# Graph attention in two layers: the opening reordered round x and the queries' weights, row sums on another engine, multiplications by zeros, a fold moved behind the second scores

## The chip, the cores and the metric

The kernel runs on one core of a Trainium2 chip. A core has a matrix engine (TensorE, PE in the profile, with its weight loads as PEld), a vector engine (VectorE, DVE), a scalar engine for activations (ScalarE, ACT), a general engine (GpSimd, POOL) and a queue that issues transfers (SyncE, SP), all working side by side and held together by semaphores. Matmul results land in PSUM, which this kernel cuts into eight banks; everything else lies in SBUF. The metric is the device time of one execution in microseconds (us), lower is better.

## The reference

The input x has 32 batches of 512 rows by 512 columns, and adj is a 512 by 512 matrix of zeros and ones. The first layer is attention with eight heads of 64, masked by adj, with a residual and a layer norm; the second multiplies by adj and by a weight matrix, again with a residual and a norm. All in float32.

```python
q = (x @ Wq + bq); k = (x @ Wk + bk); v = (x @ Wv + bv)      # split into 8 heads of 64
scores = einsum('bihd,bjhd->bhij', q, k) / sqrt(64)
weights = softmax(scores + where(adj == 0, -1e9, 0), axis=-1)
x = layernorm(x + einsum('bhij,bjhd->bihd', weights, v))
y = einsum('nm,bmd->bnd', adj, x)
x = layernorm(x + einsum('bnd,do->bno', y, weight) + bias)
```

## The kernel before

**Order.** The order of all instructions is written out by hand: each engine runs its own list in the order of the program text, and SP issues its transfers in that order too. `run(units)` simply calls a list of units one after the other. Tiles come from pools with a fixed number of buffers; a tile waits for the last reader of the buffer that it takes. PSUM banks go round in a ring of eight.

**Projections.** A projection multiplies 512 by 512 matrices by Strassen's scheme in Winograd's form: seven products of half-size blocks instead of eight. The left side's sums of blocks (S1, S2, S3, S4) lie in the tile `xT`, which holds x turned over; the right side's sums (T1, T2, T3, T4) lie in the weight tile (`wq`, `wk`, `wv`, `w1`). `sum_weights(w, n)` (L319) makes one of the four weight sums on VectorE: n = 0 makes T1, n = 1 makes T3, n = 2 makes T2, n = 3 makes T4, and T2 reads T1. `combine` makes all four and subtracts the halves of the bias (L326). `combine_rows` (L331 to L333) makes S2, S3 and S4 on POOL. `project(b, which, i)` does product i (L369, four matmuls, eight records in the trace, two for each) and takes the result out of its bank: products 1 and 5 with the bias (L394 on ACT for q and k, L391 on DVE for v), the others by additions on DVE (L397, L399, L404), with two additions on POOL after product 7 (L400, L401). The products come in the order 1, 5, 6, 7, 2, 3, 4. Product 5 reads S1 and T1, 6 reads S2 and T2, 7 reads S3 and T3, 3 reads S4, 4 reads T4; 1 and 2 read no sums.

**The opening.** SP issues, in this order: the four blocks of x's first batch (`xin`), the two halves of `wq`, `bq_c`, the two halves of `wk`, `bk_c`, `adj_s` (in the tile yT), the two halves of `wv`, `bv_r`, sixteen small transfers for the second batch (`load_squares(1)`, which need the four `xin` buffers back), the residual rows of batch 0 (`xs`), `w1`, `b1_r` and the rows of batch 1. PE turns each block of x over (`x_transpose`: four transposes, L342; eviction on ACT, L344; S1 for blocks 2 and 3 on DVE, L346), then runs the projections of batch 0, with `combine(wq)` ahead of them, `combine(wk)` after the first five products and `combine(wv)` after nine. Between them lie the transposes of adj (L301, L302, L303). The last units of the opening are the first scores, the rest of v, and the postponed additions of exponentials.

**Attention.** The heads are worked on in pairs (hp), two pairs to a group (b, g), two groups to a batch. `scores` does, for each pair and each of four blocks, two matmuls (L568), two masked copies out of the banks on DVE (L570) and one exponential on ACT (L572); POOL adds the exponentials up in `es` (L583). `attend` multiplies them by v (L592). `fold_squares` turns `es` over on DVE (L623, into a tile named e with eight buffers) and sums it (L625) into `part`; `add_up` makes the row sums across partitions on PE (L633) and their inverses on DVE (L636, L637) and POOL (L638). `turn_out` turns the result over on DVE (L606, into one of two buffers named attT) and has SP write it into `rows` by sixteen transfers (L611). `scale_rows` and `add_rows` later scale and add these.

The main loop goes through the groups: for each of the two pairs attend, fold and turn out, then the next group's scores, `add_up`, then the group's slot, a list of units made of the next batch's projections with other work merged between them. In the first group, `flips(1)` (four transposes on DVE, L353, and the sums on POOL) runs after the first pair. In the second group's slot of batch 0 lie four looks at adj (L308 on ACT, L310 and L311 on DVE), whose scratch tile is attT too.

Of the kernel before, what the change touches and what calls it, by code (L numbers as in the profile page):

```python
# [37 lines left out]
FP = mybir.dt.float32  # L38
# [3 lines left out]
AF = mybir.ActivationFunctionType  # L42
# [5 lines left out]
P = 128  # L48
# [8 lines left out]
A_AT = {"A11": 0, "A12": 1, "A21": 2, "S3": 2, "A22": 3, "S1": 4, "S2": 5, "S4": 6}  # L57
# [7 lines left out]
def load_row(nc, pool, v, name):  # L65
    t = pool.tile([P, v.shape[0]], FP, name=name)
    nc.sync.dma_start(t, bass.AP(tensor=v.tensor, offset=v.offset, ap=[[0, P], [1, v.shape[0]]]))
    return t


def load_col(nc, pool, v, name):
    t = pool.tile([P, v.shape[0] // P], FP, name=name)
    nc.sync.dma_start(t, v.rearrange("(c p) -> p c", p=P))
    return t
# [133 lines left out]
def fast_kernel(ctx: ExitStack, tc, verdict, x, adj, Wq, bq, Wk, bk, Wv, bv, W1, b1, out):  # L208
    nc = tc.nc
    B, N, D = x.shape  # L210
    H = Wq.shape[1] // HD
    HP = H // 2
    NB = N // P
# [4 lines left out]
    consts = ctx.enter_context(tc.tile_pool(name="consts", bufs=1))  # L218
    work = ctx.enter_context(tc.tile_pool(name="work", bufs=2))
# [3 lines left out]
    def bank(*shape):  # L223

        return psum.tile([P, *shape], FP, name="bank", tag="bank", bufs=8)
# [3 lines left out]
    half = N // 2  # L229

    def load(b):
        X[b] = work.tile([P, NB, D], FP, name="xT" if b == B - 1 > 1 else "xs", bufs=1 if b == B - 1 > 1 else 2)
        nc.sync.dma_start(X[b], x[b].rearrange("(c p) d -> p c d", p=P))
# [7 lines left out]
    def load_squares(b):  # L241


        for d in range(DB):
            IN[b, d] = work.tile([P, N // SQ, SQ], FP, name="xin", bufs=XIN)
            for i in range(P // SQ):
                cols = x[b, :, d * P + i * SQ:d * P + (i + 1) * SQ]
                nc.sync.dma_start(IN[b, d][i * SQ:(i + 1) * SQ, :, :], cols.rearrange("(j r) f -> r j f", r=SQ))

    def load_factors(w, name):  # L250
        t = consts.tile([P, 7, 2, half], FP, name=name)
        for s in range(2):
            nc.sync.dma_start(t[:, 2 * s:2 * s + 2, :, :].rearrange("p a c f -> p (a c) f"),
                              w[:, s * half:(s + 1) * half].rearrange("(c p) f -> p c f", p=P))
        return t

    load_blocks(0)
    wq = load_factors(Wq, "wq")
    bq_c = load_col(nc, consts, bq, "bq_c")
    wk = load_factors(Wk, "wk")  # L260
    bk_c = load_col(nc, consts, bk, "bk_c")
    adj_s = work.tile([P, NB, N], FP, name="yT", bufs=1)
    nc.sync.dma_start(adj_s, adj.rearrange("(c p) m -> p c m", p=P))
    wv = load_factors(Wv, "wv")
    bv_r = load_row(nc, consts, bv, "bv_r")
    if B > 1:
        load_squares(1)
    load(0)
    w1 = load_factors(W1, "w1")
    b1_r = load_row(nc, consts, b1, "b1_r")  # L270
    if B > 1:
        load(1)

    ident = consts.tile([P, P], FP, name="ident")
    make_identity(nc, ident)
    ones = consts.tile([P, 1], FP, name="ones")
# [37 lines left out]
    XT, QT, KT, V = {}, {}, {}, {}  # L314

    def sum_weights(w, n):

        b11, b21, b12, b22, t1, t2, t4 = (w[:, i, :, :] for i in range(7))
        nc.vector.tensor_sub(*((t1, b12, b11), (b12, b22, b12), (t2, b22, t1), (t4, b21, t2))[n])  # L319

    def combine(w, bias):

        for n in range(4):
            sum_weights(w, n)
        width = bias.shape[1] // 2
        nc.vector.tensor_sub(bias[:, width:], bias[:, width:], bias[:, :width])  # L326

    def combine_rows(t):

        a11, a12, a21, _, s1, s2, s4 = (t[:, i, :, :] for i in range(7))  # L330
        nc.gpsimd.tensor_sub(s2, s1, a11)  # L331
        nc.gpsimd.tensor_sub(a21, a11, a21)
        nc.gpsimd.tensor_sub(s4, a12, s2)  # L333

    def x_transpose(b, c):

# [18 lines left out]

    def sum_rows(b):
        xt = XT[b]
        if b:
            nc.gpsimd.tensor_add(xt[:, A_AT["S1"], :, :], xt[:, A_AT["A21"], :, :], xt[:, A_AT["A22"], :, :])
        combine_rows(xt)  # L360

    def block_product(pm, t, w, i, turned=False):
# [43 lines left out]
    def flips(b):  # L406

        return [(turn_squares if b else x_transpose, b, c) for c in range(NB)] + [(sum_rows, b)] if b < B else []

    def projections(b):  # L410


        if b >= B:
            return []
        units = [(project, b, which, i) for which in "qkv" for i in ORDER]
        for n in (5, 12):
            units[n:n + 4] = units[n + 2:n + 4] + units[n:n + 2]
        return units
# [166 lines left out]
    def attend(b, hp):  # L585
        po = bank(N)
        for j in range(NB):
            e = E.pop((b, hp, j))
            for s in range(2):
                h = 2 * (hp % 2) + s  # L590
                values = V[b][hp // 2][:, j, h * HD:(h + 1) * HD]
                nc.tensor.matmul(po[s * HD:(s + 1) * HD, :], values, e[:, s, :],  # L592
                                 start=(j == 0), stop=(j == NB - 1))
        if (b, hp // PAIRS) != (B - 1, HP // PAIRS - 1):
            SQUARES[b, hp] = work.tile([P, 2, N], FP, name="e", bufs=8)
        OUT[b, hp] = po

    def turn_out(b, hp):
# [29 lines left out]
    def add_up(b, g):  # L628

        part = PART.pop((b, g)).rearrange("p h (j i) -> p i j h", i=P // SQ)  # L630
        pm = bank(NB, GROUP)
        for i in range(P // SQ):
            nc.tensor.matmul(pm[i * SQ:(i + 1) * SQ, :, :], fold, part[:, i, :, :], start=True, stop=True,  # L633
                             tile_position=(0, i * SQ))
        inverse = INVERSE[b, g] = work.tile([P, NB, GROUP], FP, name="inverse")
        nc.vector.reciprocal(inverse, pm)  # L636
        nc.vector.tensor_add(sums, pm, sums)  # L637
        nc.gpsimd.tensor_add(inverses, inverses, inverse)  # L638
# [39 lines left out]
    def run(units):  # L678
        for unit in units:
            unit[0](*unit[1:])  # L680

    run(flips(0))
    combine(wq, bq_c)
    first = projections(0)
    run(first[:5])
    combine(wk, bk_c)
    run(first[5:9])
    combine(wv, bv_r)
    for c in range(NB):
# [74 lines left out]
    for i, (b, g) in enumerate(groups):  # L764
        for hp in range(g * PAIRS, (g + 1) * PAIRS):
            attend(b, hp)
            if i < len(groups) - 1:
                fold_squares(b, hp)
            turn_out(b, hp)
            if i == hp == 0:  # L770
                run(flips(1))
        if g == 0:
            slots = units_of(b)
        if i < len(groups) - 1:
            later = scores(*groups[i + 1])
            add_up(b, g)
        if g == 0 and b + 2 < B:
            load_squares(b + 2)
        for unit in slots[g]:
            run([unit])  # L780
            if unit[0] == convolve or unit[0] == project and unit[3] == 7:
                run(later)
                later = []
        run(later)
        later = []
# [83 lines left out]
```

## Time and profile before

| | us |
|---|---|
| median of three runs | 2764.36 (2764.18 to 2764.61) |
| the profiled execution | 2764.78 |
| span of the profiled execution, first to last instruction | 2762.9 |
| first transposes of x begin on PE | 3.71 |
| first product begins | 8.47 |
| wk's second product begins | 22.38 |
| first scores begin on PE | 41.58 |
| second scores begin on PE | 64.56 |
| PE waits for the values of batch 1 | 126.35 to 131.02 |

The profile's page gives the busy time of each engine, a picture of the span in slices, the transfers, the chain of work that ended last, and the costliest groups of instructions. The trace behind it can be asked for the instructions of any stretch in order of time, for groups by line, and for the busy time and clock of each engine in a stretch. A line of the page names source line, engine, operation, the tile written and the tiles read, how many, busy time and mean length, and the idle time before them with what ended it. The landing of each transfer is a semaphore event: the four blocks of x had landed at 3.58, 4.20, 5.80 and 6.87, the halves of wq at 8.34 and 9.78, bq_c at 10.48, the halves of wk at 11.96 and 13.59.

The last part of the page lists the transfers (tile from tensor, queue, count, size of one, us from issue to landing):

```profile
xin<-in_x_dram SPq DMA_DIRECT2D x4, 256.0 KB, 3.6
wq<-in_L_gnn_Wq_dram SPq DMA_DIRECT2D x2, 512.0 KB, 6.2
wk<-in_L_gnn_Wk_dram SPq DMA_DIRECT2D x2, 512.0 KB, 8.2
yT<-in_adj_dram SPq DMA_DIRECT2D x1, 1024.0 KB, 7.9
```

### The profile page before, as it was taken

What the parts mean: (1) busy time and instruction counts of PE and PEld (TensorE: products, weight loads), DVE (VectorE), ACT (ScalarE), POOL (GpSimd) and SP (SyncE); (2) the same over time, 40 slices, a digit from 0 to 9 for tenths busy, and PEclk for the clock granted to TensorE, in tenths of its full rate; (3) what the DMA queues carried; (4) which work ended last, traced back from release to release, by engine and by line L of the source; (5) the groups of instructions that cost most, each with busy time, mean ns of one, the idle gap of its engine ahead of it and who ended that gap; (6) DMA issues with size and microseconds to landing.
All of it is one profiled execution on the core that took longest, in us unless ns stands there. A gap on an engine that the chain in (4) does not pass through costs nothing.

```text
span 2762.9 us, 39328 instructions
## 1 busy us (share of the span) xinstructions
PE 2735.6 (99%) x12842; PEld 1912.7 (69%) x12842; DVE 2068.2 (75%) x3347; ACT 1411.1 (51%) x2459; POOL 1902.6 (69%) x1223
## 2 busy tenths in 40 slices
PE   9999999999999999999999999999999999999997
PEld 6666766767767667677676676776766767767665
DVE  6777777787777777777777777777777777787777
ACT  2455544655545546445554465454554544655554
POOL 4666777667767667676677776776666867667774
PEclk9999999999999999999999999999999999999999
DMA  5122212222122222122221222211222212222121
GB/s 147 29 31 57 45 30 56 60 60 56 25 49 58 61 56 36 38 56 62 58 53 21 56 59 60 56 26 48 58 62 57 44 30 56 61 58 57 26 51 49
DMA packets 592915, 142.20 MB, mean 51 GB/s; under 512 B 554560, under 2 KB 558656, under 8 KB 592704
## 3 DMA queue, kind: packets, MB, share of 16 engines
q1 hardware_dynamic: 592704, 139.63, 23.1%
q8 instruction: 103, 1.69, 0.3%
q14 instruction: 108, 0.88, 0.1%
HBM read 72.88 MB, written 33.55 MB: 39 GB/s over the span
## 4 chain that ended last, share of the span: by engine, by line
PE 97%; DVE 1%; SPq 1%; ACT 0%; DMA 0%; issue 0%; POOL 0%; DVEq 0%; ACTq 0%
PE bank L369 55%; PE bank L568 16%; PE bank L592 16%; PE bank L488 8%; SPq L611 1%; PE bank L633 0%; DVE bnst L431 0%; DMA wq<-in_L_gnn_Wq_dram 0%; ACT rows L649 0%; PE bank L515 0%; DVE xT L541 0%; DVE part L816 0%; DVE xs L541 0%; DVE xT L506 0%; DVE low L503 0%
## 5 line engine op out<-in xcount | busy, mean ns | idle before, releaser
L572 ACT ACTIVATE e<-e 128x1024 f32<-128x1024 f32 x512 | 524.6, 1053 | 581.3 <-DVE e L570 559.5
L570 DVE SCALAR_TENSOR_TENSOR e<-gap,bank 128x512 f32<-128x512 uint8 x1024 | 617.9, 681 | 20.2 <-PE bank L568 20.2
L583 POOL TENSOR_TENSOR es<-es,e 128x1024 f32<-128x1024 f32 x256 | 618.2, 2415 | 20.1
L583 POOL TENSOR_TENSOR es<-e 128x1024 f32<-128x1024 f32 x128 | 315.9, 2468 | 333.0 <-ACT e L572 333.0
L568 PE MATMUL bank<-q,k 64*128 64x512 f32 x2048 | 465.2, 599 | 0.0
L592 PE MATMUL bank<-e,v 128*64 128x512 f32 x2048 | 456.5, 598 | 4.7 <-DVE v L404 4.7
L369 PE MATMUL bank<-wv,xT 128*128 128x256 f32 x1792 | 405.4, 381 | 0.0
L369 PE MATMUL bank<-xT,wk 128*128 128x256 f32 x1792 | 403.0, 379 | 0.7 <-DVE wk L319 0.7
L369 PE MATMUL bank<-xT,wq 128*128 128x256 f32 x1792 | 403.1, 383 | 0.4 <-DMA wq<-in_L_gnn_Wq_dram 0.4
L369 PE MATMUL bank<-w,yT 128*128 128x256 f32 x1792 | 392.3, 379 | 0.5 <-DVE yT L520 0.5
L568 PEld LDWEIGHTS bank<-q,k 64*128 64x128 f32 x2048 | 204.0, 186 | 259.6 <-issue 160.4
L369 PEld LDWEIGHTS bank<-w,yT 128*128 128x128 f32 x1792 | 340.0, 190 | 48.1 <-DVE yT L520 0.9
L369 PEld LDWEIGHTS bank<-xT,wk 128*128 128x128 f32 x1792 | 340.2, 190 | 47.2 <-PE bank L369 1.1
L369 PEld LDWEIGHTS bank<-xT,wq 128*128 128x128 f32 x1792 | 339.5, 191 | 47.4 <-ACT xT L344 0.8
L369 PEld LDWEIGHTS bank<-wv,xT 128*128 128x128 f32 x1792 | 337.5, 190 | 47.5 <-DVE e L570 0.8
L649 ACT ACTIVATE rows<-rows,zero,inverse 128x64 f32<-128x64 f32 x1008 | 343.2, 427 | 0.0
L592 PEld LDWEIGHTS bank<-e,v 128*64 128x64 f32 x2048 | 142.2, 137 | 283.8 <-issue 282.7
L653 POOL TENSOR_TENSOR xs<-xs,rows 128x512 f32<-128x512 f32 x124 | 158.4, 1289 | 168.0 <-DMA xs<-in_x_dram 168.0
L572 ACT ACT_TABLE_LOAD x30 | 38.5, 1283 | 423.9 <-DVE e L570 423.9
L461 DVE TENSOR_TENSOR low<-xs,high 128x512 fp32r<-128x512 f32 x122 | 143.5, 1176 | 104.2 <-ACT high L457 104.2
L446 ACT ACTIVATE xs<-xs,shift,rstd 128x512 f32<-128x512 f32 x248 | 181.9, 803 | 32.5 <-DVE shift L441 32.5
L541 DVE TENSOR_TENSOR xs<-bank,xs 128x512 f32<-128x512 f32 x186 | 124.5, 683 | 96.9 <-PE bank L369 46.5
(122 smaller groups left out, 2970.1 us busy)
## 6 DMA issues: line engine op xcount, KB each, us to landing
rows<-attT SPq DMA_DIRECT2D x2016, 16.0 KB, 1.8
xin<-in_x_dram SPq DMA_DIRECT2D x496, 64.0 KB, 2.5
xs<-in_x_dram SPq DMA_DIRECT2D x31, 1024.0 KB, 5.2
out_dram<-xs SPq DMA_DIRECT2D x31, 1024.0 KB, 4.4
xin<-in_x_dram SPq DMA_DIRECT2D x4, 256.0 KB, 3.6
wq<-in_L_gnn_Wq_dram SPq DMA_DIRECT2D x2, 512.0 KB, 6.2
wk<-in_L_gnn_Wk_dram SPq DMA_DIRECT2D x2, 512.0 KB, 8.2
yT<-in_adj_dram SPq DMA_DIRECT2D x1, 1024.0 KB, 7.9
```

Source lines behind the costliest of these rows:

```text
L369: nc.tensor.matmul(pm[:, r, :], left[:, d, r * P:(r + 1) * P], right[:, d, :], start=(d == 0), stop=(d == 1))
L446: nc.scalar.activation(row, row, AF.Identity, bias=SHIFT[t][:, slot:slot + 1], scale=RSTD[t][:, slot:slot + 1])
L461: nc.vector.tensor_sub(LOW[b, d], cols, HIGH[b, d].bitcast(FP))
L488: nc.tensor.matmul(pm.rearrange("p a n -> p (a n)"), part, adjT[:, n % NB, :], start=(n == 0), stop=(n == 2 * NB - 1))
L541: nc.vector.tensor_add(block, pm, block)
L568: nc.tensor.matmul(ps[s], keys[:, j * P:(j + 1) * P], queries, start=True, stop=True)
L570: nc.vector.scalar_tensor_tensor(e[:, s, :], gap[:, j, :], NEG * root, ps[s], op0=ALU.mult, op1=ALU.add)
L572: nc.scalar.activation(e, e, AF.Exp, scale=1.0 / root)
L583: nc.gpsimd.tensor_add(ES[b, hp], ES[b, hp] if j > 1 else E[b, hp, 0], E[b, hp, j])
L592: nc.tensor.matmul(po[s * HD:(s + 1) * HD, :], values, e[:, s, :], start=(j == 0), stop=(j == NB - 1))
L649: nc.scalar.activation(part, part, AF.Identity, bias=zero, scale=inverse[:, c, s:s + 1])
L653: nc.gpsimd.tensor_add(cols, cols, ROWS.pop((b, hp)))
```

## The change

Five things change; what is computed does not.

1. Seven matmuls of a 128 by 128 tile of zeros (`still`) with itself stand at the head of PE's list. VectorE sets the tile to zero. Nothing reads their result.
2. Only x's first blocks and wq (and bq_c) are issued at once. Every other transfer is issued later in the program text, and the first of them, wk, has to wait: ScalarE writes one column of the tile wk after the eviction of x's third block, and the transfer overwrites it.
3. The row sums S2, S3, S4 of the first batch are made on VectorE, alternating with the weight sums in the order T1, S2, T2, S3, T3, S4; T4 and the bias follow after the first product, and wk's T1 is made after the third, ahead of the other wk sums. S1 of the first batch is still made by `x_transpose`.
4. In the first group, the second pair's fold moves behind the second scores; it writes into a buffer named v (three buffers) in place of e.
5. In the first group, `add_up` moves into the slot, in front of its ninth unit (after five projections of batch 1).

```diff
--- before.py
+++ after.py
@@ -247,8 +247,9 @@
                 cols = x[b, :, d * P + i * SQ:d * P + (i + 1) * SQ]
                 nc.sync.dma_start(IN[b, d][i * SQ:(i + 1) * SQ, :, :], cols.rearrange("(j r) f -> r j f", r=SQ))
 
-    def load_factors(w, name):
-        t = consts.tile([P, 7, 2, half], FP, name=name)
+    def load_factors(w, name, t=None):
+        if t is None:
+            t = consts.tile([P, 7, 2, half], FP, name=name)
         for s in range(2):
             nc.sync.dma_start(t[:, 2 * s:2 * s + 2, :, :].rearrange("p a c f -> p (a c) f"),
                               w[:, s * half:(s + 1) * half].rearrange("(c p) f -> p c f", p=P))
@@ -256,21 +257,6 @@
 
     load_blocks(0)
     wq = load_factors(Wq, "wq")
-    bq_c = load_col(nc, consts, bq, "bq_c")
-    wk = load_factors(Wk, "wk")
-    bk_c = load_col(nc, consts, bk, "bk_c")
-    adj_s = work.tile([P, NB, N], FP, name="yT", bufs=1)
-    nc.sync.dma_start(adj_s, adj.rearrange("(c p) m -> p c m", p=P))
-    wv = load_factors(Wv, "wv")
-    bv_r = load_row(nc, consts, bv, "bv_r")
-    if B > 1:
-        load_squares(1)
-    load(0)
-    w1 = load_factors(W1, "w1")
-    b1_r = load_row(nc, consts, b1, "b1_r")
-    if B > 1:
-        load(1)
-
     ident = consts.tile([P, P], FP, name="ident")
     make_identity(nc, ident)
     ones = consts.tile([P, 1], FP, name="ones")
@@ -318,19 +304,18 @@
         b11, b21, b12, b22, t1, t2, t4 = (w[:, i, :, :] for i in range(7))
         nc.vector.tensor_sub(*((t1, b12, b11), (b12, b22, b12), (t2, b22, t1), (t4, b21, t2))[n])
 
-    def combine(w, bias):
-
-        for n in range(4):
+    def combine(w, bias, which=range(4)):
+
+        for n in which:
             sum_weights(w, n)
         width = bias.shape[1] // 2
         nc.vector.tensor_sub(bias[:, width:], bias[:, width:], bias[:, :width])
 
-    def combine_rows(t):
+    def combine_rows(t, engine=nc.gpsimd, which=range(3)):
 
         a11, a12, a21, _, s1, s2, s4 = (t[:, i, :, :] for i in range(7))
-        nc.gpsimd.tensor_sub(s2, s1, a11)
-        nc.gpsimd.tensor_sub(a21, a11, a21)
-        nc.gpsimd.tensor_sub(s4, a12, s2)
+        for n in which:
+            engine.tensor_sub(*((s2, s1, a11), (a21, a11, a21), (s4, a12, s2))[n])
 
     def x_transpose(b, c):
 
@@ -355,8 +340,7 @@
 
     def sum_rows(b):
         xt = XT[b]
-        if b:
-            nc.gpsimd.tensor_add(xt[:, A_AT["S1"], :, :], xt[:, A_AT["A21"], :, :], xt[:, A_AT["A22"], :, :])
+        nc.gpsimd.tensor_add(xt[:, A_AT["S1"], :, :], xt[:, A_AT["A21"], :, :], xt[:, A_AT["A22"], :, :])
         combine_rows(xt)
 
     def block_product(pm, t, w, i, turned=False):
@@ -592,7 +576,9 @@
                 nc.tensor.matmul(po[s * HD:(s + 1) * HD, :], values, e[:, s, :],
                                  start=(j == 0), stop=(j == NB - 1))
         if (b, hp // PAIRS) != (B - 1, HP // PAIRS - 1):
-            SQUARES[b, hp] = work.tile([P, 2, N], FP, name="e", bufs=8)
+
+            late = (b, hp) == (0, 1)
+            SQUARES[b, hp] = work.tile([P, 2, N], FP, name="v" if late else "e", bufs=3 if late else 8)
         OUT[b, hp] = po
 
     def turn_out(b, hp):
@@ -679,11 +665,42 @@
         for unit in units:
             unit[0](*unit[1:])
 
-    run(flips(0))
-    combine(wq, bq_c)
-    first = projections(0)
-    run(first[:5])
-    combine(wk, bk_c)
+
+    still = work.tile([P, N], FP, name="attT")[:, 0:P]
+    nc.vector.memset(still, 0.0)
+    pm = bank(P)
+    for _ in range(7):
+        nc.tensor.matmul(pm, still, still, start=True, stop=True)
+    turned, first = flips(0), projections(0)
+    run(turned[:3])
+
+    wk = consts.tile([P, 7, 2, half], FP, name="wk")
+    nc.scalar.activation(wk[:, 0, 0, 0:1], zero, AF.Copy)
+    bq_c = load_col(nc, consts, bq, "bq_c")
+    load_factors(Wk, "wk", wk)
+    bk_c = load_col(nc, consts, bk, "bk_c")
+    adj_s = work.tile([P, NB, N], FP, name="yT", bufs=1)
+    nc.sync.dma_start(adj_s, adj.rearrange("(c p) m -> p c m", p=P))
+    wv = load_factors(Wv, "wv")
+    bv_r = load_row(nc, consts, bv, "bv_r")
+    if B > 1:
+        load_squares(1)
+    load(0)
+    w1 = load_factors(W1, "w1")
+    b1_r = load_row(nc, consts, b1, "b1_r")
+    if B > 1:
+        load(1)
+    run(turned[3:NB])
+
+    for n in (0, 2, 1):
+        sum_weights(wq, n)
+        combine_rows(XT[0], nc.vector, ({0: 0, 2: 1, 1: 2}[n],))
+    run(first[:1])
+    combine(wq, bq_c, (3,))
+    run(first[1:3])
+    sum_weights(wk, 0)
+    run(first[3:5])
+    combine(wk, bk_c, (1, 2, 3))
     run(first[5:9])
     combine(wv, bv_r)
     for c in range(NB):
@@ -764,7 +781,7 @@
     for i, (b, g) in enumerate(groups):
         for hp in range(g * PAIRS, (g + 1) * PAIRS):
             attend(b, hp)
-            if i < len(groups) - 1:
+            if i < len(groups) - 1 and (i or hp == 0):
                 fold_squares(b, hp)
             turn_out(b, hp)
             if i == hp == 0:
@@ -773,7 +790,11 @@
             slots = units_of(b)
         if i < len(groups) - 1:
             later = scores(*groups[i + 1])
-            add_up(b, g)
+            if i:
+                add_up(b, g)
+            else:
+                fold_squares(b, 1)
+                slots[0].insert(8, (add_up, b, g))
         if g == 0 and b + 2 < B:
             load_squares(b + 2)
         for unit in slots[g]:
```

## The prediction

> **What bounds the kernel now.** I read the busy table and the slices first, then the chain of waits, then the opening and the stretch round 126 us in the timeline.
>
> ```profile
> PE 2735.6 (99%) x12842; PEld 1912.7 (69%) x12842; DVE 2068.2 (75%) x3347; ACT 1411.1 (51%) x2459; POOL 1902.6 (69%) x1223
> ```
>
> TensorE (PE) is busy 2735.6 of 2762.9 us and ends the chain (97%). From 140 to 2723 us its matmuls follow one another without a gap, so nothing is won there; and work taken from other engines counts only where PE waits or runs slowly. The chain, in order of time (start, length, what), names the places:
>
> ```profile
> 2.60 5.73 DMA wq<-in_L_gnn_Wq_dram
> ...
> 8.47 11.47 PE bank L369 x40
> ...
> 20.57 1.68 DVE wk L319
> ...
> 41.65 7.14 PE bank L568 x32
> ...
> 64.63 8.64 PE bank L568 x32
> ```
>
> The first product waits for the first half of wq; 0.73 us go at 21.65 to 22.38 while VectorE makes a sum of wk; and the second scores take 8.64 us where the first, with the same matmuls, take 7.14. PE's pace is the third loss. Groups by form for 8.4 to 13.5 us, then for 14 to 19.8 us (count, busy us, mean ns):
>
> ```profile
> L369 PE MATMUL bank<-xT,wq 128*128 128x256 f32 x12 | 5.3, 634 | 0.4 <-DMA wq<-in_L_gnn_Wq_dram 0.4
> ...
> L369 PE MATMUL bank<-xT,wq 128*128 128x256 f32 x28 | 6.3, 382 | 0.0
> ```
>
> The same matmuls start every 0.43 us at first, every 0.216 us later: half clock up to 13.54 us, where the trace's clock record has its first change (the windows view prints 1.00 before it, having no record there). Later the record shows a half clock twice (windows: us, PE busy, others, clock, DMA):
>
> ```profile
> 126.00:129.60 3.60, 0.33 (x2) 0.00 (x0) 1.76 (x3) 0.61 (x2) 3.46 (x2) 1.00 0.06 9
> 129.60:136.40 6.80, 5.38 (x14) 1.89 (x16) 6.73 (x11) 2.67 (x9) 4.92 (x3) 0.50 0.01 1
> ...
> 2727.10:2730.50 3.40, 2.92 (x7) 2.37 (x8) 2.14 (x4) 1.46 (x3) 1.66 (x1) 0.50 0.02 5
> ```
>
> Both follow a wait of PE: 4.68 us at 126.35 (VectorE's L310 waits until 127.80 for the row transfers that read attT, and the values queue behind it) and 3.96 us at 2723.62. All changes lie whole multiples of 3.413 us apart.
>
> **What the Trainium skill says.** "TensorE: Matmul & The Clock Gate", Part 1, gives this: half clock by default and after an idle window of about 3.4 us, full clock after a busy one, windows free-running. The trace agrees: windows 75% and 76% busy (3.30 to 6.71, 6.71 to 10.12) did not release it, one 87% busy (2727.13 to 2730.55) did, one 95% idle took it away. Part 4 of the page says that transposes don't count as busy in the same way; here both low windows hold transposes, so the trace can't tell. "DMA: Bandwidth & Descriptors", Queues, rings and completion order: each ring consumes its descriptors in order. So bytes issued after wq should hardly delay wq: by the packets, all 1024 one-kilobyte packets of wq have begun at about 8.7 us, and only the slow rings (second half landed 8.49 to 9.78) shared the end with wk. "GPSIMD Engine Reference", Specifications: its SBUF interfaces are shared with VectorE, contended by two-input operations. The trace agrees: L319 takes 0.69 us alone, up to 1.75 beside the row sums of GpSimd (POOL).
>
> **The change, part by part**, against the profiled execution (2764.78 us: span 2762.9 and 1.9 around it; 0.42 above the median 2764.36).
>
> Zeros. VectorE's memset (some 0.2 us, as the ident memset on POOL), then seven 128-column fp32 matmuls from about 1.0 us. A 256-column one takes 0.85 us at half clock (two records of 0.43), so 0.43 each and 3.0 together, to 4.0. The first block of x lands at 3.58, so its transposes start 0.3 late; hidden, as the third block lands at 5.80 and needs 16 x 0.213 us in all. PE is then busy 1.0 to 5.7 without a hole and again until about 7.7; the window 3.30 to 6.71 is some 97% busy. If all of it counts, full clock from 6.71 at this phase, before 7.7 at nearly any.
>
> Transfers held. wk waits for a ScalarE write placed behind the third block's eviction (7.00 to 7.60), so it is issued at about 7.9 instead of 4.18; bq_c keeps its place. Queued behind on SP: wk, bk_c, adj, wv, bv_r, the 16 squares of x, xs, w1, b1. SP reached adj at 8.65 before[...]; now about 10. With the rings drained, wk lands near its old 11.96 and 13.59; the rest 0.5 to 1.5 later. Needs, new scale: wk at 15.3, adj at 24 (landed 16.54), wv at 25 (landed 20.2), squares at 58 (last issued at 27.36). All covered; without cover every us costs one. For wq: no gain, or up to 0.9 (a standstill of the packets at 4.24 to 5.2 begins with wk's issue, perhaps by chance). I take 8.34 as before for the first half and 9.5 for the second.
>
> Sums. Rows and weights now alternate on VectorE, 0.69 each without POOL beside them: T1 first. First product 8.47 to 10.20 at full clock (8 records of 0.216 = 1.73). T1: 9.5 + 0.10 + 0.69 + 0.08 = 10.37, the second product's start, a new 0.17 wait. S2 and T2 are ready 1.4 later, S3 and T3 2.8 later; products follow at 1.73 and 3.45. Then T4, the bias and q's addition until 15.5, and wk's first sum by 16.2. The fourth product after the second, and then wk's first, end at 10.37 + 5 x 1.73 = 19.0: wk's second product starts there instead of 22.38, without the 0.73 wait. Gain 3.4 (ends: 4.5 with wq 0.9 earlier; 3.1 with wq as before; 0.7 if the clock stays low). POOL loses three operations that nothing else waits for.
>
> Fold. Between the last values and the second scores VectorE had the first fold, attT, four x transposes (to 64.3), the second fold (1.20 + 1.22) and attT (0.71): L570 starts at 67.26, 2.7 after PE, all eight banks fill and PE then follows VectorE's 0.60 pace. Without that fold it starts at about 65.7, the 1.15 after PE that the first scores show, and these run in 7.14. Gain 1.5 (at least 0, at most 1.6). The fold comes after the scores: VectorE is free at 65.7 + 9.62 + 2.42 = 77.7 instead of 77.0 (with add_up's two small operations, which move behind the fifth projection). PE, 1.5 ahead, has eight banks; VectorE waited 3.96 us in this stretch (before 87.58), which hides it.
>
> What the sums don't touch: the 4.68 us wait. L310 waits for transfers that begin with attT of the third pair (104.92), itself 0.2 behind PE; it moves along rigidly. Its clock loss does not. Before, PE resumed at 131.02 and ran at half until 136.42: 2.7 lost. Shifted by 4.9 on the same windows, it resumes at 126.1, half clock from 126.18 to 129.59: 1.7 lost. Gain 1.0, bounds -0.7 to 2.7 (released late, not dropped at all). The tail lost 1.5; shifted it may lose 0 to 2.8. I take it as unchanged.
>
> Sum: 3.4 + 1.5 + 1.0 = 5.9; 2764.78 - 5.9 = 2758.9 for such a profiled execution, **2758.5** against the median.
>
> **Rivals.** *Zeros without effect.* Transposes don't count and three us of zeros don't fill a window: half clock until about 13.5. Then 0.7 (wk's wait) + 0.2 (phase) + 1.5, and a later clock worth 0.5 in the middle of its bounds: 2764.4 - 2.9 = 2761.5. For it: the skill's Part 4; against: no busier window of this kind was there to fail. *Both later drops gone.* The windows are split by the waits at 121 and 2718, PE keeps full clock: 4.9 + 2.7 + 1.5 = 9.1, or 7.4 if only the tail is spared; I put it at 2756.0. For it: 4.68 and 3.96 us are barely more than one window; against: the spread of only 0.43 us over three runs says that the phase repeats, and on it the first drop stays. *The held queue comes late.* One mechanism, on SP: all transfers behind wk stay late by their hold, wv's sums block VectorE's queue in front of the k additions, and PE waits. Slack of wv is 25 - 20.2 = some 4.5 us; beyond that each us costs one; from 9.4 on it eats the 4.9, and at 15 the time is 2770. Against it: the hold is 3.7 us at most, and SP was held[...].
>
> **How the numbers follow.** A difference under 0.2% (5.5 us) is about what a measurement of this kernel can tell from no change. Forecast 55%, zeros without effect 25%, both drops gone 16%, late queue 4%. The range 2755.6 to 2762.2 takes in the first three's bounds. Over 0.2% faster means under 2758.8, which halves the forecast: 0.33 of its 0.55, 0.16 and 0.03 give 0.52; 0.44 within; 0.04 slower.
>
> **What would show it.** Right: products of wq at 380 ns from 8.5 us on; wk's second product starting at about 19.0; L568 at 7.1 to 7.2 us for the second scores near 60; a 4.7 us wait near 121. Wrong: means over 600 ns after 9 us (zeros); wq landing under 7.6 or wk beyond 15.3 (transfers); L568 still over 8 us, or PE waits between 68 and 85 (fold); SP-released waits of PE before 60.

## The result, and the profile after

The median is 2760.32 us (2759.26 to 2762.28, 20 runs) against 2764.57 for the kernel before (2763.43 to 2765.93, 20 runs), measured alongside: 4.25 us less, a ratio of 0.9984 with the interval [0.9978, 0.9991]. The forecast was 2758.5 in a range of 2755.6 to 2762.2; the time lies in the range. The gain is 0.15%; the prediction gave 0.52 to one of over 0.2%, and 0.44 to a change of less than that. The profiled execution took 2760.76 us: a span of 2758.2 and 2.6 around it (before: 2762.9 and 1.9).

The page of the kernel after, with the busy table, three groups of section 5 (count | busy us, mean ns | idle before, releaser) and two transfers of section 6 (count, KB each, us from issue to landing). In the new file the products' line is L353 (was L369), the scores' L552 (L568), the values' L576 (L592), the weights' sums L305 (L319), the looks L296 (L310) and the eviction of masked scores L554 (L570).

```profile
PE 2733.3 (99%) x12856; PEld 1912.9 (69%) x12856; DVE 2065.3 (75%) x3351; ACT 1411.5 (51%) x2460; POOL 1898.7 (69%) x1220
...
L552 PE MATMUL bank<-q,k 64*128 64x512 f32 x2048 | 463.6, 598 | 0.0
L576 PE MATMUL bank<-e,v 128*64 128x512 f32 x2048 | 456.5, 598 | 4.7 <-DVE v L388 4.7
...
L353 PE MATMUL bank<-xT,wq 128*128 128x256 f32 x1792 | 400.8, 381 | 2.2 <-DMA wq<-in_L_gnn_Wq_dram 1.8
...
wq<-in_L_gnn_Wq_dram SPq DMA_DIRECT2D x2, 512.0 KB, 7.0
wk<-in_L_gnn_Wk_dram SPq DMA_DIRECT2D x2, 512.0 KB, 5.1
```

PE is 2.3 us less busy although it has 14 more instructions: it ran at half clock for less time (up to 6.62 us of the opening, not up to 13.54). Its idle time before the first product grew (1.8 us of the 2.2, 0.4 before), because the transposes end sooner while wq lands no earlier; wq took 7.0 us from issue to landing where it took 6.2.

The chain of waits of after (start, length, what), to be held against that of before:

```profile
3.08 7.52 DMA wq<-in_L_gnn_Wq_dram
10.70 0.70 DVE wq L305
11.44 14.08 PE bank L353 x64
...
39.37 7.14 PE bank L552 x32
...
62.35 7.21 PE bank L552 x32
```

The first thing that binds is now the second half of wq (landed at 10.60), then one sum, and from 11.44 on 64 records of products (eight products) without a hole. Scores start at 39.30 instead of 41.58, and the second ones take 7.21 us instead of 8.64.

The timeline of PE in the same execution (start, length, line, count, idle before):

```profile
1.06 3.36 PE L673 MATMUL bank<-attT 128*128 128x128 f32 x14 [1.06 <-DVE attT L670]
4.21 3.11 PE L327 MATMUL bank<-ident,xin 128*128 128x128 f32 x16
9.12 1.97 PE L353 MATMUL bank<-xT,wq 128*128 128x256 f32 x8 [1.80 <-DMA wq<-in_L_gnn_Wq_dram]
11.44 7.17 PE L353 MATMUL bank<-xT,wq 128*128 128x256 f32 x32 [0.35 <-DVE wq L305]
```

Eight records in 1.97 us are full clock from the first product on. In the groups by form from 9.1 to 14 us the same matmuls, at 634 ns before, read:

```profile
L353 PE MATMUL bank<-xT,wq 128*128 128x256 f32 x20 | 4.8, 388 | 2.2 <-DMA wq<-in_L_gnn_Wq_dram 1.8 <-DVE wq L305 0.4
```

Where the time went between the two profiled executions, from the starts of PE's groups: 2.28 us are won by the first scores, another 1.24 between the second scores (62.28, was 64.56) and the third (104.72, was 108.24), so 3.5. From there to the sums that follow the fourth scores (144.87, was 148.38) nothing is won or lost. By the last gap of PE (2719.27, was 2723.62) it is 4.35; the 0.84 us between come little by little over 2575, most of them in the multiplications by adj, and some 0.7 of them belong to the change too (e2). The tail after the gap took 26.29 us, as before (26.33).

### The profile page after: what moved, and what is told of

Same layout as the page of the kernel before. It is cut to its first block, busy times and chain, and to the rows that moved or that the text cites. A ratio compares the mean times of both kernels' runs of the same rounds, so it can differ in the third digit from the quotient of the medians.

```text
span 2758.2 us, 39360 instructions
## 1 busy us (share of the span) xinstructions
PE 2733.3 (99%) x12856; PEld 1912.9 (69%) x12856; DVE 2065.3 (75%) x3351; ACT 1411.5 (51%) x2460; POOL 1898.7 (69%) x1220
## 4 chain that ended last, share of the span: by engine, by line
PE 97%; DVE 1%; SPq 1%; ACT 0%; DMA 0%; issue 0%; POOL 0%; DVEq 0%; ACTq 0%
PE bank L353 55%; PE bank L552 16%; PE bank L576 16%; PE bank L472 8%; SPq L597 1%; PE bank L619 0%; DMA wq<-in_L_gnn_Wq_dram 0%; DVE bnst L415 0%; ACT rows L635 0%; PE bank L499 0%; DVE xT L525 0%; DVE part L837 0%; DVE xs L525 0%; DVE xT L490 0%; DVE stat L416 0%
## 5 line engine op out<-in xcount | busy, mean ns | idle before, releaser
L554 DVE SCALAR_TENSOR_TENSOR e<-gap,bank 128x512 f32<-128x512 uint8 x1024 | 617.8, 678 | 20.6 <-PE bank L552 20.6
L552 PE MATMUL bank<-q,k 64*128 64x512 f32 x2048 | 463.6, 598 | 0.0
L576 PE MATMUL bank<-e,v 128*64 128x512 f32 x2048 | 456.5, 598 | 4.7 <-DVE v L388 4.7
L353 PE MATMUL bank<-wv,xT 128*128 128x256 f32 x1792 | 405.4, 381 | 0.0
L353 PE MATMUL bank<-xT,wq 128*128 128x256 f32 x1792 | 400.8, 381 | 2.2 <-DMA wq<-in_L_gnn_Wq_dram 1.8
L353 PE MATMUL bank<-xT,wk 128*128 128x256 f32 x1792 | 402.9, 379 | 0.0
L353 PE MATMUL bank<-w,yT 128*128 128x256 f32 x1792 | 392.3, 379 | 0.5 <-DVE yT L504 0.5
L552 PEld LDWEIGHTS bank<-q,k 64*128 64x128 f32 x2048 | 203.1, 186 | 258.9 <-issue 149.2
L353 PEld LDWEIGHTS bank<-w,yT 128*128 128x128 f32 x1792 | 340.0, 190 | 48.3 <-DVE yT L504 0.9
L353 PEld LDWEIGHTS bank<-xT,wk 128*128 128x128 f32 x1792 | 340.2, 190 | 46.1
L353 PEld LDWEIGHTS bank<-xT,wq 128*128 128x128 f32 x1792 | 337.8, 190 | 49.1 <-issue 2.0
L353 PEld LDWEIGHTS bank<-wv,xT 128*128 128x128 f32 x1792 | 337.5, 190 | 47.6 <-DVE e L554 0.8
L576 PEld LDWEIGHTS bank<-e,v 128*64 128x64 f32 x2048 | 142.2, 137 | 283.8 <-issue 282.7
```

The source lines that it names most:

```text
L353: nc.tensor.matmul(pm[:, r, :], left[:, d, r * P:(r + 1) * P], right[:, d, :], start=(d == 0), stop=(d == 1))
L552: nc.tensor.matmul(ps[s], keys[:, j * P:(j + 1) * P], queries, start=True, stop=True)
L554: nc.vector.scalar_tensor_tensor(e[:, s, :], gap[:, j, :], NEG * root, ps[s], op0=ALU.mult, op1=ALU.add)
```

## The experiments

All of them change the kernel after, except two that put one part into the kernel before. Medians, with that of the kernel before as measured alongside, and three stretches of each profile: L, from the landing of wq's second half to wk's second product; F, from the second scores to the third; G, from the third scores to the sums after the fourth.

| kernel | us | before | ratio [95%] | wq's halves landed | L | F | G |
|---|---|---|---|---|---|---|---|
| before | 2764.57 | | | 8.34, 9.78 | 12.60 | 43.68 | 40.15 |
| after | 2760.32 | 2764.57 | 0.9984 [0.9978, 0.9991] | 8.99, 10.60 | 9.58 | 42.44 | 40.15 |
| a0_again | 2760.51 | 2764.92 | 0.9985 [0.9978, 0.9991] | 8.72, 10.22 | 9.59 | 42.44 | 40.14 |
| e1_no_zeros | 2761.25 | 2765.04 | 0.9987 [0.9980, 0.9994] | 8.97, 10.38 | 12.08 | 42.44 | 40.16 |
| e2_no_hold | 2761.29 | 2765.04 | 0.9987 [0.9981, 0.9994] | 8.84, 10.45 | 9.58 | 42.43 | 40.13 |
| e3_fold_back | 2761.21 | 2765.04 | 0.9988 [0.9981, 0.9994] | 8.64, 10.15 | 9.58 | 43.67 | 40.15 |
| e4_rows_pool | 2762.92 | 2765.04 | 0.9994 [0.9986, 1.0003] | 9.09, 10.59 | 11.68 | 42.43 | 40.16 |
| e5_look | 2757.22 | 2764.92 | 0.9975 [0.9965, 0.9986] | 7.95, 9.39 | 9.59 | 42.43 | 38.21 |
| e7_turned | 2760.28 | 2764.92 | 0.9984 [0.9977, 0.9991] | 8.56, 10.05 | 10.77 | 42.44 | 40.14 |
| e8_before_zeros | 2764.98 | 2764.92 | 1.0001 [0.9993, 1.0010] | 9.33, 11.00 | 10.98 | 43.67 | 40.15 |
| e6_bq_late | 2759.81 | 2764.62 | 0.9983 [0.9976, 0.9990] | 8.12, 9.52 | 9.59 | 42.43 | 40.13 |
| e9_before_fold | 2763.64 | 2764.62 | 0.9996 [0.9988, 1.0004] | 8.48, 9.84 | 12.67 | 42.44 | 40.14 |
| e10_looks_early | 2751.46 | 2764.62 | 0.9951 [0.9937, 0.9965] | 9.04, 10.69 | 9.59 | 42.44 | 31.35 |

The landing of wq differs by 1.4 and 1.6 us among these executions (by 1.0 to 1.3 us both among those that hold the other transfers back and among those that don't), and all that follows shifts with it. L, F and G are free of that: where the program doesn't differ in the stretch they repeat within 0.1 us. So the parts are read from them first.

**e1: without the zeros.**

```diff
-    still = work.tile([P, N], FP, name="attT")[:, 0:P]
-    nc.vector.memset(still, 0.0)
-    pm = bank(P)
-    for _ in range(7):
-        nc.tensor.matmul(pm, still, still, start=True, stop=True)
```

> The changed kernel without the seven matmuls of zeros (their result is read by nothing). Theory 'clock': half clock until the first window full of products ends, about 13.5 us on the grid of the two traces; products of wq start every 0.43 us from about 9 us, wk's second product starts near 21.7 instead of 20.2, so 1.5 us are lost at the first scores. Theory 'zeros do nothing' (the transposes alone release the clock, or the sums alone made the gain): release still near 6.6, second product within 0.5 of 20.2. On the later wait of 4.7 us: it would begin near 124.3; if the clock windows keep their grid (ends at 126.1 and 129.5), the loss there is between 0 and 1.7 instead of 2.7, so the total is 2759.0 to 2761.8 against 2760.3.

Groups by form of PE from 9.1 to 14 us in this kernel:

```profile
L353 PE MATMUL bank<-xT,wq 128*128 128x256 f32 x12 | 5.5, 645 | 1.2 <-DMA wq<-in_L_gnn_Wq_dram 1.2
```

645 ns against 388: half clock, here until 15.02, and L is 2.5 us longer. Zeros do release the clock: in the nine traces with them it was free between 3.97 and 7.20, each time ahead of the first product. The median says less: without them the gain over before is 3.79 us, 0.5 to 0.6 less than the 4.25 and 4.41 of the two measurements of after. A release at 15.02 is a late one (11.36 and 13.54 in the two traces with the opening of before, which have no zeros either), and each us of half clock costs half a us (records of products start every 0.43 us in place of 0.216), so one trace can overstate the zeros by an us or more. This execution took 2762.78, the second longest of 21 and 1.5 above their median; whether that is the whole difference isn't settled.

**e8: the zeros alone, in the kernel before.** The five lines of e1's diff stand ahead of `run(flips(0))`.

> The kernel before with the seven matmuls of zeros alone. Theory 'clock and sums pay only together': full clock by 8 us, but T1, T2 and wk's T1 come late as in the run with the sums on GpSimd; from the first product to wk's second 13.0 us, against 13.9 in the kernel before, the first scores gain under 1 us, total within 1 us of the kernel before. Rival 'the clock is the gain': 11.1 us, first scores 2.3 us earlier, total 2.3 us lower.

The median doesn't move (1.0001). The clock was free from 4.09, and yet the trace's shorter L comes mostly from elsewhere. The timeline of GpSimd in this trace (lines as in before; start, length), where wq's second half landed late, at 11.00:

```profile
8.04 1.26 POOL L331 TENSOR_TENSOR xT<-xT 128x512 f32<-128x512 f32 x1 [5.58 <-DVE xT L346]
9.26 1.26 POOL L332 TENSOR_TENSOR xT<-xT 128x512 f32<-128x512 f32 x1
10.49 1.27 POOL L333 TENSOR_TENSOR xT<-xT 128x512 f32<-128x512 f32 x1
```

and VectorE's sums of wq, first in this kernel, then in the kernel before:

```profile
11.10 3.25 DVE L319 TENSOR_TENSOR wq<-wq 128x512 f32<-128x512 f32 x4 [3.14 <-DMA wq<-in_L_gnn_Wq_dram]
```

```profile
9.88 5.20 DVE L319 TENSOR_TENSOR wq<-wq 128x512 f32<-128x512 f32 x4 [0.76 <-DMA wq<-in_L_gnn_Wq_dram]
```

GpSimd's row sums were nearly over when wq came, so VectorE's four sums took 3.25 us instead of 5.20. When wq lands at its usual time the sums lie beside the row sums, and then the products wait for them at either clock: the opening of before has L 12.60 with the clock released at 13.54, and 12.67 (e9) with it released at 11.36. Behind slow sums a fast clock was worth nothing here.

**e4: the sums back on GpSimd and VectorE as before, zeros and hold kept.**

```diff
-    for n in (0, 2, 1):
-        sum_weights(wq, n)
-        combine_rows(XT[0], nc.vector, ({0: 0, 2: 1, 1: 2}[n],))
-    run(first[:1])
-    combine(wq, bq_c, (3,))
-    run(first[1:3])
-    sum_weights(wk, 0)
-    run(first[3:5])
-    combine(wk, bk_c, (1, 2, 3))
+    combine_rows(XT[0])
+    combine(wq, bq_c)
+    run(first[:5])
+    combine(wk, bk_c)
```

> The changed kernel with the first batch's row sums on GpSimd again and all of wq's and wk's sums in the old order. Theory: at full clock the old sums are late: T2 at about 13.6, so the third product waits some 0.4 us, and wk's T1 makes its second product wait 0.5 to 1.2 us as before; wk's second product near 21.4 instead of 20.2, 1.2 lost at the first scores. Rival 'the sums were never on the path': second product within 0.3 of 20.2.

Timeline of PE:

```profile
9.23 1.97 PE L353 MATMUL bank<-xT,wq 128*128 128x256 f32 x8 [1.46 <-DMA wq<-in_L_gnn_Wq_dram]
12.04 2.00 PE L353 MATMUL bank<-xT,wq 128*128 128x256 f32 x8 [0.84 <-DVE wq L305]
14.40 5.42 PE L353 MATMUL bank<-xT,wq 128*128 128x256 f32 x24 [0.37 <-DVE wq L305]
...
22.27 1.97 PE L353 MATMUL bank<-xT,wk 128*128 128x256 f32 x8 [0.73 <-DVE wk L305]
```

Every product is at full clock and PE waits three times for a sum, 0.84 + 0.37 + 0.73 = 1.94 us, of which only 0.35 is left in after. L grows by 2.1 us, and the median by as much (a gain of 2.12 us instead of 4.25). With e9 below the medians add up: the fold 1.0, then 2.8 more for the sums and the later transfers (e1 against e9; e2 puts some 0.7 of it on the transfers, which leaves the 2.1 of here for the sums), the zeros on top 0.5 to 0.6, together 4.3 to 4.4. So the sums on VectorE are the largest part, and the zeros, worth nothing alone (e8), pay beside them.

**e2: the transfers not held back.** Their calls stand right behind wq's, and ScalarE's mark in wk is gone:

```diff
     wq = load_factors(Wq, "wq")
+    wk = consts.tile([P, 7, 2, half], FP, name="wk")
+    bq_c = load_col(nc, consts, bq, "bq_c")
+    load_factors(Wk, "wk", wk)
...
-    nc.scalar.activation(wk[:, 0, 0, 0:1], zero, AF.Copy)
```

> The changed kernel with the other transfers issued at once in the old order, without the ScalarE write that holds wk. Theory 'hold brings nothing': wq's halves land within 0.8 us of 8.99 and 10.60 (as they scatter from run to run), wk's second product starts within 0.8 of 20.2, total within 1 us of 2760.3. Rival 'hold carries the start': wq lands over 1 us later, second product at 21.2 or later, total 2761.5 or more. Rival 'hold harms' (wq landed 0.65 and 0.82 later with it in the two profiles): wq lands near 8.3 and 9.8, second product near 19.4, total near 2759.5.

L is 9.58 either way, wq landed at 8.84 and 10.45, wk at 12.06 and 13.51 (after: 12.18 and 13.66; before: 11.96 and 13.59). The hold neither brings wq forward nor makes wk late. Yet the gain over before is 3.75 us, 0.5 to 0.7 less than the two of after. Those were measured at other times, so the medians don't decide at that size, but the traces do. From the fifth scores to the last the nine kernels whose transfers are held take 2491.55 to 2491.71 us, and the four without it (before, e8, e9 and this one) 2492.32 to 2492.53, without an overlap. Groups by form of PE from 180 to 2660 us, in e2 and then in after:

```profile
L487 PE MATMUL bank<-adjT,low 128*128 128x512 f32 x472 | 140.2, 418 | 0.0
L487 PE MATMUL bank<-adjT,high 128*128 128x512 f32 x472 | 129.2, 395 | 0.0
```

```profile
L472 PE MATMUL bank<-adjT,low 128*128 128x512 f32 x472 | 140.0, 418 | 0.0
L472 PE MATMUL bank<-adjT,high 128*128 128x512 f32 x472 | 128.8, 394 | 0.0
```

The multiplications by adj are 0.6 us shorter in after, and PE's other groups with equal counts agree within 0.1. So issuing the transfers later is worth some 0.7 us, not in the opening but spread over all batches. Why isn't known: the edit also changes when and in what order the tiles of these transfers (wk, yT, wv, w1 and others) are set up, and no run separates this from the hold.

**e6: bq_c behind wk.** It asked whether the small packets of bq_c slow wq's end.

```diff
-    bq_c = load_col(nc, consts, bq, "bq_c")
     load_factors(Wk, "wk", wk)
+    bq_c = load_col(nc, consts, bq, "bq_c")
```

> The changed kernel with bq_c issued behind wk instead of ahead of it. Its 512 four-byte pieces go over the rings just when wq's second half ends (8 to 9.5 us, at 170 to 250 GB/s in place of 350). Theory 'bq_c's pieces delay wq': second half lands 0.5 to 1 us earlier than 10.2 to 10.6 and wk's second product follows, at 18.9 to 19.4; q's first eviction waits for bq_c at about 14 instead and costs nothing; total lower by 0.5 to 1. Rival: the landing scatters as before (second half 9.4 to 10.6 in eight traces), no change of the total beyond 0.5.

wq landed at 8.12 and 9.52, which is early, but e5 without this edit has 7.95 and 9.39; the gain over before is 4.81 us, 0.4 to 0.6 more than after's, which was measured at another time. Inconclusive.

**e3 and e9: the fold put back, and the fold alone in before.** e3 undoes this, and e9 does it in the kernel before (which has no `late`; the lines are e3's, turned round):

```diff
-            late = False
+            late = (b, hp) == (0, 1)
...
-            if i < len(groups) - 1:
+            if i < len(groups) - 1 and (i or hp == 0):
                 fold_squares(b, hp)
...
-            add_up(b, g)
+            if i:
+                add_up(b, g)
+            else:
+                fold_squares(b, 1)
+                slots[0].insert(8, (add_up, b, g))
```

> The changed kernel with the second fold and add_up back where they were. Theory: second scores take 8.6 us again instead of 7.2, and the shift against the kernel before at the third scores is 2.3 instead of 3.5 us, so 1.2 lost there. Rival 'the fold only moved the work': same shift of 3.5 there. The wait for the values would begin near 124.0; on the clock's grid no window is then wholly idle (60% and 77%), so if those do not take the full clock away, 2.7 us come back and the total is 2758.9; if they do, it is 2761.5.

> The kernel before with the fold and add_up moved as in the change, and nothing else of it. Theory: from the second scores to the third 42.44 us as in all kernels with the moved fold, against 43.68 in those without; total 1.2 lower than before, 2763.5 on a chip where before is 2764.7, if the wait of 4.7 us and its half clock stay. Rival 'the opening has to be early for it': no change of that stretch.

The second scores, in the timeline of PE in e3 and then in e9:

```profile
61.84 8.71 PE L552 MATMUL bank<-q,k 64*128 64x512 f32 x32
```

```profile
64.69 7.28 PE L568 MATMUL bank<-q,k 64*128 64x512 f32 x32
```

F is 43.67 to 43.68 in all three traces with the fold ahead of the scores and 42.43 to 42.44 in the ten others: 1.24 us, whatever else is changed. Alone it moved the median by 0.98; putting it back cost 0.4 to 0.6 of the gain (3.83 left of 4.25 or 4.41, measured at other times).

**a0: the same kernel again.**

> The changed kernel once more, beside the others on one chip. Theory: the clock windows lie anew in every execution (their ends fell at 3.3, 3.2, 1.4, 1.3, 2.8 and 0.6 us modulo 3.413 in six traces), so the shift at the third scores is 3.5 within 0.8 as wq's landing scatters, and the half clock after the 4.7 us wait lasts 0, 3.4 or 6.8 us by chance. Total 2760.3 within 0.7.

L, F and G repeat to 0.02 us. What differs is wq's landing, the clock's release (6.05 against 6.62) and the place of the later drop. The ends of the clock's windows, taken modulo 3.413 us, lay at 3.30 in before, 3.21 in after, 1.37 in e1, 1.33 in e2, 2.83 in e3 and 0.56 in e4: the phase differs from execution to execution, here too (2.63 in a0, the same kernel as after).

**e5: the look without its wait.** `look_for_low_half` writes its difference over the copy it reads instead of into a fresh attT buffer, so that nothing waits for the row transfers.

```diff
-        cut = work.tile([P, N], FP, name="attT")
+        cut = kept.bitcast(FP)
```

> The changed kernel with one line of look_for_low_half changed: the comparison is written over the tile that it reads (two buffers of its own) instead of into attT. Theory: the 4.7 us wait of PE near 123 us ends with the row transfers that read attT, so without that buffer the wait goes and with it the half clock behind it; total lower by 4.7 plus 1.7 to 3.4, near 2753.5. Rival 'something else is late just behind' (the values wait for the ScalarE copies or for GpSimd's sums, which queue there too): a wait of over 1 us stays at the same place, total above 2756.

The timeline of PE in e5:

```profile
119.67 7.26 PE L576 MATMUL bank<-e,v 128*64 128x512 f32 x32
126.86 2.85 PE L552 MATMUL bank<-q,k 64*128 64x512 f32 x12
131.23 1.12 PE L552 MATMUL bank<-q,k 64*128 64x512 f32 x2 [1.52 <-DVE attT L592]
134.23 7.56 PE L552 MATMUL bank<-q,k 64*128 64x512 f32 x18 [1.88 <-DVE attT L592]
```

The 4.7 us wait is gone, yet G falls only from 40.15 to 38.21. Two waits for VectorE come in its place, and a half clock from 133.49 on. (The median fell by 3.1 to 3.3 us against after's, more than this trace's G; why wasn't followed up.) This says what really holds the stretch: VectorE. Behind the values' evictions, with the four looks woven in, it has four x transposes, two folds and two attT to do before the next sixteen of L554.

**e10: the looks moved too.** e5's edit, and the four looks go from the slot ahead of those scores into the first slot, where VectorE has idle time:

```diff
+            behind += [[(look_for_low_half, c)] if c is not None else [] for c in (0, 1, None, None, 2, 3)]
...
-        looked = [(look_for_low_half, c) for c in range(NB)] if b == 0 else []
+        looked = []
```

> The changed kernel with the looks at adj writing over their own tile (as in the run without the attT buffer) and moved into the first group's slot, behind the sixth, seventh, tenth and eleventh product, where VectorE waited 3.8 us and then 1 us per product. Theory: the 4.7 us wait is gone as there, and so are the waits of 1.5 and 1.9 us behind it, which came from VectorE being late with four transposes, two folds and attT after the looks; no half clock between 20 us and the tail; total near 2751. Rival 'that queue is late anyway' (the folds wait for GpSimd's sums): waits of over 1 us near 130 stay, total above 2754.

Its timelines of PE and of VectorE:

```profile
120.98 7.09 PE L576 MATMUL bank<-e,v 128*64 128x512 f32 x32
127.99 8.24 PE L552 MATMUL bank<-q,k 64*128 64x512 f32 x32
136.17 0.26 PE L619 MATMUL bank<-part,fold 128*32 128x16 f32 x8
```

```profile
130.23 9.62 DVE L554 SCALAR_TENSOR_TENSOR e<-gap,bank 128x512 f32<-128x512 uint8 x16
```

No wait and no half clock here; G is 31.35, 8.8 us shorter, and the median 2751.46 (2750.23 to 2751.73, 5 runs), 13.2 under before and 8.9 under after. This version beats both.

**e7: transposes in place of the zeros.** The two lines that make `still` go as well.

```diff
-    for _ in range(7):
-        nc.tensor.matmul(pm, still, still, start=True, stop=True)
+    for _ in range(14):
+        nc.tensor.transpose(pm, ident, ident)
```

> The changed kernel with fourteen transposes of the identity in place of the seven matmuls of zeros, some 3.0 us of PE too, from about 1.4 us on. Theory 'transposes count for the clock': release by 8 us, wk's second product 11.0 to 11.2 us after the first product begins, as with zeros. Rival (the skill's remark that transposes do not count as busy in the same way): release only at 11.9 to 15.4 us, second product about 13.3 us after the first one begins, as without zeros.

The windows view of e7, then of after, each cut at the ends of the clock's own windows (stretch, PE busy and records, the other engines, PEclk, DMA share, GB/s):

```profile
2.05:5.46 3.41, 3.41 (x18) 3.41 (x17) 0.00 (x0) 0.00 (x0) 0.42 (x5) 1.00 0.94 301
5.46:8.88 3.42, 1.62 (x14) 1.33 (x13) 0.85 (x2) 2.16 (x5) 0.00 (x0) 1.00 1.03 323
8.88:12.29 3.41, 3.41 (x9) 2.70 (x9) 2.14 (x4) 0.00 (x0) 0.00 (x0) 0.50 0.97 286
```

```profile
3.21:6.62 3.41, 3.41 (x18) 3.37 (x17) 0.00 (x0) 1.06 (x2) 0.00 (x0) 1.00 0.90 291
6.62:10.03 3.41, 1.61 (x10) 1.28 (x9) 0.85 (x2) 1.31 (x4) 0.00 (x0) 1.00 1.01 296
```

PEclk is printed as 1.00 in the first line of each only because the record begins at its end. A window that held nothing but transposes released the clock at 5.46. The next one, 47% busy, took it away again for 3.41 us, and L grew by 1.2; in after a window as busy by the view (47%) kept it. e7's was busy mainly with transposes (until 6.90), that of after more than half with products, and a less busy window of products alone kept it in e8 (7.51 to 10.92: 1.45 us of 3.41, 43%). So transposes may weigh less once the clock is up; two or three windows don't prove it. The median equals after's.

## Why the prediction was right, and where it was not

The number alone would not have told: 2760.32 lies 1.8 us from the forecast and 1.2 from the rival in which the zeros do nothing (2761.5). The traces do.

**Zeros: right in their effect.** Full clock at 6.62 where 6.71 was worked out; that close by luck of the phase, but ahead of 7.7, as said, in all nine traces with the zeros. The Trainium skill's page "TensorE: Matmul & The Clock Gate", Part 4, holds that transposes don't count as busy in the same way; e7's release at 5.46 behind transposes alone shows that they can suffice here, so that was no ground for the rival in which the zeros fail. The prediction's shares for its two low windows were too low: by the windows view PE is busy for 2.80 and 2.97 of 3.41 us there, 82% and 87% in place of 75% and 76%, and the later window that did release has 2.97 of 3.42, 87% too. The share alone didn't part them. And what the zeros are worth came out smaller than the steps imply: between a low clock (a gain of 0.7) and a released one (3.4) lay 2.7 us; e1's one trace puts 2.5 on the zeros and its median 0.5 to 0.6.

**Sums: right.** From the second half of wq to wk's second product the working has 19.0 - 9.5 = 9.5 us; measured 9.58. **The landing was mis-sized**: it was taken as 8.34, as before, and 9.5 (9.78 before) and came at 8.99 and 10.60, inside a scatter of 7.95 to 9.33 and 9.39 to 11.00 over thirteen traces. So wk's second product started at 20.18 instead of 19.0, and 2.2 us were won instead of 3.4. The bounds of the step (0.7 to 4.5) held this, though for a reason of clock, not of landing.

**Transfers held: as said for the waits, but with a worth that was put at nothing.** wk landed at 13.66, before its need at 15.3, and PE waited for no later transfer than wq in the opening; the late-queue rival is refuted. The standstill of packets looks like chance, as allowed for: from 4.5 to 5.0 us before moved 121 GB/s, and the three other kernels that issue wk at once (e2, e8, e9) 285 to 365. Missing is the 0.7 us of e2, in the multiplications by adj, where the prediction saw nothing to win because PE has no gap there.

**Fold: right mechanism, 1.24 for 1.5.** L554 follows PE by 1.23 us (63.51 after 62.28) as said, and the scores run in 7.21; they are 1.43 shorter. The other 0.2 goes back at the new place of add_up: the wq products behind these scores took 8.83 us instead of 8.74 (e3), and the next sixteen of wk 3.56 instead of 3.45.

**The clock behind the 4.68 us wait: the step that failed.** It put 1.0 us on 1.7 us of loss instead of 2.7. Two things were wrong. The phase doesn't repeat, so the spread of three runs was no evidence (that before and after have nearly the same phase, 3.30 and 3.21, was luck). And the loss costs nothing: the drop lies on PE, but VectorE is later. The timelines of PE in after (half clock 126.08 to 132.91) and in e2 (half clock 127.63 to 131.05), from the wait's end to the sums:

```profile
127.50 8.04 PE L576 MATMUL bank<-e,v 128*64 128x512 f32 x24 [4.69 <-DVE v L388]
135.47 9.47 PE L552 MATMUL bank<-q,k 64*128 64x512 f32 x32
144.87 0.26 PE L619 MATMUL bank<-part,fold 128*32 128x16 f32 x8
```

```profile
127.35 7.07 PE L591 MATMUL bank<-e,v 128*64 128x512 f32 x24 [4.68 <-DVE v L403]
134.34 3.70 PE L567 MATMUL bank<-q,k 64*128 64x512 f32 x14
138.90 5.88 PE L567 MATMUL bank<-q,k 64*128 64x512 f32 x18 [0.86 <-DVE attT L607]
144.71 0.26 PE L634 MATMUL bank<-part,fold 128*32 128x16 f32 x8
```

With the shorter drop the values are 1.0 us shorter and the scores start earlier, then PE waits 0.86 for attT. The sums come 17.37 and 17.36 us after the wait's end. VectorE's own timeline in after has no hole from 124.65 to

```profile
138.93 9.62 DVE L554 SCALAR_TENSOR_TENSOR e<-gap,bank 128x512 f32<-128x512 uint8 x16
```

and this start follows the third scores by 34.21 us in before (142.44) and in after alike. G is 40.13 to 40.16 in eleven traces, with drops of 3.41 and of 6.83 us. The prediction asked what is late next when a stall goes, but not when a slow stretch goes. The rival with both drops gone counted 2.7 us here as well.

**Tail: as taken**, 26.29 us for 26.33; over all traces 25.85 to 27.02 with the phase.

**The sum.** 2.2 + 1.24 + 0 in place of 3.4 + 1.5 + 1.0 is 3.5 of 5.9. The profiled pair differs by 4.0: the stretch behind, mostly the multiplications by adj, adds 0.84, and the end of the span, after PE's last matmul, 0.4, while 0.7 more is spent outside the span. That the time lies in the range is in part luck: a sum that was 2.4 too high and a term that was missing go opposite ways, and the range is 6.6 us wide.

## What to carry over

Before pricing a slow or idle stretch of the bounding engine, look for the engine that comes next in the same stretch: here VectorE's queue made a drop of the clock free, took back, in the trace, more than half of a 4.7 us wait that was removed, and let the gain through only when its own work was moved to an idle slot. A warm-up of the clock pays only if the operands are ready at the faster pace, so price the sums and transfers in front of it first. Compare stretches measured from the event that starts them, such as a landing, since absolute starts carry that event's scatter. And before a small steady difference is called scatter, sort all traces by what they share: here it followed one part of the change.

## What the runs showed of the hardware

The two 512 KB transfers of wq landed up to 1.4 and 1.6 us apart from one execution to another, over thirteen, and by 1.0 to 1.3 with the others held back and without. The clock's windows lay at another phase in each execution. Every 4.7 us wait of PE was followed by a half clock of 3.41 or 6.83 us, as the Trainium skill's page "TensorE: Matmul & The Clock Gate", Part 1, has it after an idle window. But the window need not be idle throughout: in e3 the one that took the clock away (122.30 to 125.71) still held 1.31 us of matmuls, 38%. Neither does a window have to be full to release it: 2.91 of 3.41 us of zeros, 85%, did (e4, 0.56 to 3.97), 2.72, 80%, did not (e5, 0.37 to 3.78). How long the clock stays half isn't fixed by the wait. And transposes alone, 3.41 us of them, released the clock (e7).
